# A six-block decoder on one core: its loads and first steps at the edges of the blocks rearranged

## The chip, the core and the metric

The kernel runs on one core of a Trainium2 chip. The core has a matrix engine (PE in the profile, with its weight loads as PEld), a vector engine (DVE), a scalar engine (ACT), GpSimd (POOL) and SyncE (SP), which here only issues DMAs. Each engine works through its own queue of instructions in order. The metric is the device time in microseconds of one execution; lower is better.

## What is computed

The input x holds 16 batches of 256 rows of 256 numbers, all in float32. Six blocks follow one another, each of the form x = x + block(layernorm(x)):

```python
x = x + L0_attn(ln(x))            # block 0: causal attention, 16 heads of 64, with biases bq, bk, bv, bo
x = x + L0_xattn(ln(x), ctx)      # block 1: attention to a context, with an additive mask, 16 heads of 64
x = x + L0_ffn(ln(x))             # block 2: RMS norm, top 2 of 8 experts, x itself added once more inside
x = x + L1_attn(ln(x))            # block 3: causal linear attention, 16 heads of 16
x = x + L1_xattn(ln(x), ctx)      # block 4: softmax attention to the same context, 16 heads of 16, biases
x = x + L1_ffn(ln(x))             # block 5:
#   gates = sigmoid(x @ w_gate), 8 per head; only the first largest is kept (gm)
#   values = einsum('bhne,ehdk,bnd->bhnk', gm, value_experts, x)
#   causal softmax attention over 8 heads of 64 with these values
#   out = einsum('bhne,ehkd,bhnk->bhnd', gm, output_experts, attended), summed over the heads
```

## The kernel before, in words

All rows of x stay in SBUF (xs, one tile of 128 x 2 x 256 for each batch). The weights rotate through three slots of 128 x 8192 floats (pool wp, line 37): first w_a (block 0, wq, wk, wv, wo at columns 0, 2048, 4096, 6144), then w_x, the experts' m_w1 and m_w2, then w34 (lines 733 to 739), which holds the weights of blocks 3 and 4 and block 5's two projections in columns 0 to 6143; columns 6144 to 8191 are unused. The last two are w_ve and w_oe of block 5. A loader of weights is load_rows (line 43), always on SP's queue.

The order in which PE works is written out by hand: each block is a loop of steps over heads and batches, under a manual schedule for PE alone. On every other engine and on SP's queue, the build decides the order from its own estimate of what is ready, with earlier program text first; so a later load may stand ahead of an earlier one in SP's queue. That queue is then fixed, and its head, waiting for a semaphore, holds all behind it.

Each stage opens its own SBUF pool and PSUM pool and closes them at its end (s01 and p01 for blocks 0 and 1, s2 for block 2, s3 for block 3, s4 for block 4, s5 for block 5). The next stage's pool takes the memory of the one before.

Start (lines 54 to 72): SP issues the load of x's first batch, then the four parts of w_a in the order wq, wk, wv, wo (line 52), then the other 15 batches of x, then the biases bq0, bk0, bv0, bq1, bk1 and the gate weights wg, then some more constants, bo0 (line 355) among them. Block 0 begins on PE with the transposes of the first batch (line 189), the values ps_v from wv (line 393), then queries and keys ps_qk (line 408), which ACT copies out with the biases (lines 414 and 417; bq0s is bq0 scaled on DVE, line 107), the scores (line 235), the softmax on DVE and ACT, its normalising on POOL (line 256), and the transposes of the probabilities (line 266). POOL also adds bo0 to each batch of x (line 374).

Block 4 needs keys and values of the context for each batch. They are computed ahead by context4 (line 287), a generator of three parts: load the batch's context ct (line 79), project the keys, copy them on ACT and store them to DRAM (kd), and the same for the values (vd). Two batches (EARLY) are done at the end of block 1, with their stores on ACT's queue. The other 14, called late, are done in block 3, with ct in two slots of the pool vep and their stores on SP's queue. fill (line 306) advances the generators: when one ends, it starts the next but one, which issues that one's load. In block 3, eight parts come before the first step, three in each of the steps -3 to -1 and one in each later step. In the text of step 10 stands load_ffn (line 891), 12 loads for block 5's weights on SP, which wait for a gate that POOL writes into the slots from batch 2's x (line 895).

Block 3 ends with the statistics of the last batch for block 4: output3, stats and rstd_one (lines 1063 to 1073), whose last operations run on POOL (lines 157 to 164).

Block 4 (lines 1126 to 1300) runs 64 sets (batch, m, o) in steps -3 to 68. prepare4 loads k4 and v4 of a batch from kd and vd into tiles of the stage pool s4, and makes the normalised rows; keys4 makes from k4, on ACT, the four masked and biased km (line 1158); project4 makes the queries; scores4 takes scores for the maxima (line 1205, reduced on DVE at 1211), maxima4 adds the maxima to the queries, exps4 takes the scores again (line 1231) and ACT exponentiates them into pT, weighted4 multiplies by the values (line 1244) and finish4 transposes and normalises (lines 1257, 920 and 924). The first DMA of the stage is the bias bv1 (line 1130). statistics5 (line 1264) makes block 5's statistics, on DVE and then POOL.

Block 5 begins with before5(0) (line 1316), in five steps of its own: transposes of the normalised rows to hT, gates on PE (ps_g), a chain of DVE operations with one exponential on ACT (lines 1328 to 1340) to gm, its transposes (line 1345), a copy and a store to DRAM (gd). Only then the first pair5 (line 1353): queries and keys, causal scores (one PSUM buffer for them, so that a pair's scores wait for the pair before to be exponentiated), expert values, and the sums, with gr loaded from gd. For later batches before5 runs beside pair5 of the batch before.

Of the kernel before, what the change touches and what calls it, by code (L numbers as in the profile page):

```python
# [10 lines left out]
F32 = mybir.dt.float32  # L11
# [6 lines left out]
P = 128  # L18
# [7 lines left out]
def decoder(ctx: ExitStack, tc: tile.TileContext, a: dict, out: bass.AP):  # L26
# [21 lines left out]
        return dst  # L48

    def load_attention(which):  # L50
        w = weights(f"w_{which}")
        return [load_rows(w, 2048 * i, f"{which}_{n}") for i, n in enumerate(("wq", "wk", "wv", "wo"))]

    xs = []
    for b in range(NB):
# [2 lines left out]
        xs.append(xb)  # L58
        if b == 0:
            w_first = load_attention("a0")  # L60

    def load_const(name, shape, src):
        t = const.tile(shape, F32, tag=name, name=name)
        nc.sync.dma_start(out=t, in_=src)
        return t

    bq0 = load_const("bq0", [P, 8], a["a0_bq"])
    bk0 = load_const("bk0", [P, 8], a["a0_bk"])
    bv0 = load_const("bv0", [P, 8], a["a0_bv"])
    bq1 = load_const("bq1", [P, 2], a["x1_bq"])  # L70
    bk1 = load_const("bk1", [P, 2], a["x1_bk"])
    wg = load_const("wg", [P, 2, 64], a["f_wg"].rearrange("(c p) e -> p c e", p=P))

    dram = ctx.enter_context(tc.tile_pool(name="dram", bufs=1, space=bass.MemoryType.DRAM))

    def ctx_rows(b, pool):

        ct = pool.tile([P, 2, S], F32, tag="c", name="c", bufs=2)
        nc.sync.dma_start(
            out=ct, in_=a["ctxT"][:, b * S : (b + 1) * S].rearrange("(c p) s -> p c s", p=P)  # L80
        )
        return ct
# [201 lines left out]
    kds = [dram.tile([P, 2, S], F32, tag=f"kd{b}", name=f"kd{b}") for b in range(NB)]  # L284
    vds = [dram.tile([P, 2, D], F32, tag=f"vd{b}", name=f"vd{b}") for b in range(NB)]

    def context4(b, pool, mm, wk, wv, kt, vt, queue, cpool=None):

        ct = ctx_rows(b, cpool or pool)
        yield  # L290
        ps = mm([P, 2, S], "ps_k4")
        for m in range(2):
            two_k(ps[:, m, :], lambda c: wk[:, c, m * P : (m + 1) * P], lambda c: ct[:, c, :])
        k = pool.tile([P, 2, S], F32, tag=kt[0], name="k4", bufs=kt[1])
        nc.scalar.copy(k, ps)
        queue.dma_start(out=kds[b], in_=k)
        yield
        ps = mm([P, 2, D], "ps_v4")
        for t in range(2):
            two_k(ps[:, t, :], lambda c: ct[:, c, t * P : (t + 1) * P], lambda c: wv[:, c, :])  # L300
        v = pool.tile([P, 2, D], F32, tag=vt[0], name="v4", bufs=vt[1])
        nc.scalar.copy(v, ps)
        queue.dma_start(out=vds[b], in_=v)
        yield

    def fill(gens, n):

        for _ in range(n):
            while gens and next(gens[0], 0) == 0:
                gens.pop(0)  # L310
                if len(gens) > 1:
                    next(gens[1])

# [29 lines left out]
    with ExitStack() as st:  # L345
# [338 lines left out]
        with tc.manual_schedule(engines={mybir.EngineType.PE}):  # L684
            prepare(0, 0)
            rows_T(0, 0)
            values(0, 0, 0)
            n = 0
            early = []
            while n < len(duos) + 4 or routing:  # L690
                if n == 2:
                    wts[1] = load_attention("x0")
                    for p in perms:
                        nc.sync.dma_start(out=p.rearrange("(p f) o -> p (f o)", p=P), in_=zero)
                if n == 4 * NB + 4:
                    load_moe()
                if n == len(duos) - 1:
                    w4 = []
                    for name, cols in (("x1_wqk", slice(D, 2 * D)), ("x1_wv", slice(0, D))):
                        w = pool.tile([P, 2, D], F32, tag="v", name="w4", bufs=6)  # L700
                        nc.sync.dma_start(
                            out=w, in_=a[name][:, cols].rearrange("(c p) e -> p c e", p=P)
                        )
                        w4.append(w)
                    early = [
                        context4(b, pool, mm_tile, *w4, ("qk", 2), ("v", 6), nc.scalar)
                        for b in range(EARLY)
                    ]
                    next(early[0])
                    next(early[1])  # L710
                step(n)
                n += 1
            fill(early, 2 * EARLY)
# [16 lines left out]
    with ExitStack() as st:  # L730
# [6 lines left out]
        wxqk = load_rows(w34, 2048, "x1_wqk")  # L737
        wxv = load_rows(w34, 3072, "x1_wv")
        wfqk = [load_rows(w34, 4096, "f_wq"), load_rows(w34, 5120, "f_wk")]

        def once(shape, name, dt=F32):
            return pool.tile(shape, dt, tag=name, name=name, bufs=1)
# [186 lines left out]
    with ExitStack() as st:  # L929
# [133 lines left out]
        def output3(b):  # L1063
# [9 lines left out]
            rstd_one(4, b, pool, nc.gpsimd)  # L1073

        late = [
            context4(b, pool, mm3, wxqk[:, :, D : 2 * D], wxv, ("k4", 2), ("v4", 2), nc.sync, vep)
            for b in range(EARLY, NB)
        ]

# [24 lines left out]
                    values3(b + 1)  # L1104

        with tc.manual_schedule(engines={mybir.EngineType.PE}):
            next(late[0])
            next(late[1])
            combine(0)
            fill(late, 8)  # L1110
            for s in range(-3, len(SETS) + 6):
                step3(s)
                fill(late, 3 if s < 0 else 1)
                if s == 10:
                    load_ffn(xs[2][0:1, 0, 0:32])

    ve_stack.close()
    rt_stack.close()

# [4 lines left out]
    with ExitStack() as st:  # L1126
# [40 lines left out]
            )  # L1167

        def prepare4(b):
            k = pool.tile([P, 2, S], F32, tag="k4", name="k4", bufs=2)  # L1170
            nc.sync.dma_start(out=k, in_=kds[b])
            v = pool.tile([P, 2, D], F32, tag="v4", name="v4", bufs=2)
            nc.sync.dma_start(out=v, in_=vds[b])
            kvs[b] = k, v
            hs4[b] = normed(4, b)

            nc.gpsimd.tensor_tensor(
# [118 lines left out]

        with tc.manual_schedule(engines={mybir.EngineType.PE}):
            prepare4(0)
            for s in range(-3, len(SETS) + 5):
                step4(s)  # L1300

# [3 lines left out]
    with ExitStack() as st:  # L1307
# [3 lines left out]
        wve = [w_ve[:, 2048 * g : 2048 * (g + 1)] for g in range(4)]  # L1311
        wve = [w.rearrange("p (k c f) -> p k c f", k=2, c=2) for w in wve]
        woe = [w_oe[:, 2048 * g : 2048 * (g + 1)].rearrange("p (e d) -> p e d", e=8) for g in range(4)]
        hTs, gms, gds, pos = {}, {}, {}, {}

        def before5(b):
            ps = transposed(normed(5, b), psum, "mm", bufs=3)
            hT = hTs[b] = hp.tile([P, 2, S], F32, tag="hT", name="hT")
            nc.scalar.copy(hT, ps)
            yield 6  # L1320

            ps = psum.tile([P, 2, 64], F32, tag="mm", name="ps_g", bufs=3)
            for t in range(2):
                two_k(ps[:, t, :], lambda c: hT[:, c, t * P : (t + 1) * P], lambda c: wg[:, c, :])
            gt = pool.tile([P, 16, 8], F32, tag="gt", name="gt")
            gtf = gt.rearrange("p a e -> p (a e)")

            nc.vector.tensor_scalar(gtf, ps.rearrange("p t e -> p (t e)"), -80.0, None, ALU.max)
            nc.scalar.activation(gtf, gtf, AF.Exp, scale=-1.0)
            nc.vector.tensor_scalar(gtf, gtf, 1.0, None, ALU.add)  # L1330
            nc.vector.reciprocal(gtf, gtf)
            m = pool.tile([P, 16], F32, tag="m", name="m")
            nc.vector.tensor_reduce(m, gt, AX.X, ALU.max)
            oh = pool.tile([P, 16, 8], F32, tag="oh", name="oh")
            nc.vector.tensor_tensor(oh, gt, m.unsqueeze(2).to_broadcast([P, 16, 8]), ALU.is_equal)
            nc.vector.tensor_tensor(oh, oh, rev.unsqueeze(1).to_broadcast([P, 16, 8]), ALU.mult)
            nc.vector.tensor_reduce(m, oh, AX.X, ALU.max)
            nc.vector.tensor_tensor(oh, oh, m.unsqueeze(2).to_broadcast([P, 16, 8]), ALU.is_equal)
            gm = gms[b] = pool.tile([P, 2, 8, 8], F32, tag="gm", name="gm")
            nc.vector.tensor_tensor(gm.rearrange("p t h e -> p (t h) e"), oh, gt, ALU.mult)  # L1340
            yield 6
            yield 6
            ps = psum.tile([64, 2, P], F32, tag="mm", name="ps_gT", bufs=3)
            for t in range(2):
                nc.tensor.transpose(
                    ps[:, t, :], gm[:, t, :, :].rearrange("p h e -> p (h e)"), ident
                )
            gmT = pool.tile([64, S], F32, tag="gmT", name="gmT")
            nc.scalar.copy(gmT, ps.rearrange("p t s -> p (t s)"))
            gd = gds[b] = dram.tile([64, S], F32, tag="gd", name="gd", bufs=2)  # L1350
            nc.sync.dma_start(out=gd, in_=gmT)

        def pair5(b, hp):
            hT, gm = hTs[b], gms[b]
            cols = slice(hp * P, (hp + 1) * P)
            ps = psum.tile([P, 2, S], F32, tag="mm", name="ps_qk", bufs=3)
            for i in range(2):
# [8 lines left out]
            for j in range(2):  # L1366
                h = 2 * hp + j
                nc.sync.dma_start(
                    out=gr[64 * j : 64 * j + 64].rearrange("p e s -> p (e s)"),
                    in_=gds[b][8 * h : 8 * h + 8, :]  # L1370
                    .rearrange("e s -> (e s)")
                    .partition_broadcast(64),
                )
# [44 lines left out]
                nc.sync.dma_start(out=out[b].rearrange("(t p) d -> p t d", p=P), in_=xs[b])  # L1418

        def steps5():  # L1420
            yield [(6, before5(0))]
            for _ in range(4):
                yield []
            for b in range(NB):
                for hp in range(4):
                    new = [(3, pair5(b, hp))]
                    if hp == 2 and b + 1 < NB:
                        new.append((6, before5(b + 1)))
                    yield new

        with tc.manual_schedule(engines={mybir.EngineType.PE}):
# [75 lines left out]
```

## Time and profile before

| | us |
|---|---|
| median of 3 runs | 3912.89 (3911.7 to 3913.84) |
| the profiled execution, device time | 3917.66 |
| its span, from its first to its last instruction | 3916.0 |
| PE busy in the span | 3759.0 |
| DVE, ACT, POOL busy | 2248.7, 1616.7, 1039.2 |

The profile's times come from the one profiled execution and are counted from the span's start. In a list in order of time each line gives the start, the duration of the group, the engine, the line of the kernel, the operation, output and inputs by the program's names, and in brackets how long the engine had been idle and what released it; "issue" there means that nothing the profile shows was waited for. A line with SPq or ACTq is a DMA's issue on that queue. In the chain of work that ended last, each line gives start, duration and what it was. In a table by stage, each engine's busy time follows the stretch and its length, and at the end come the granted clock of PE, the share of DMA time and GB/s. Block 3 begins at about 2017, block 4 at about 2384, block 5 at about 2719. From 2770 to 3890 PE is busy all the time.

### The profile page before, as it was taken

How to read it: one execution, taken by the hardware profiler on the slowest of the kernel's cores; microseconds unless marked ns; L12 is line 12 of the kernel's file. 1: busy time of each engine (PE TensorE's matmuls, PEld its weight loads, DVE VectorE, ACT ScalarE, POOL GpSimd, SP SyncE). 2: the span in 40 equal slices, each digit the busy share in tenths (PEclk: the TensorE clock that was granted, in tenths of full speed). 3: DMA queues.
4: the chain of work that ended last, by engine and by line, in shares of the span. 5: the costliest groups of instructions: out<-in, count | busy, mean ns of one | idle time of the engine just before them, and what ended most of it. 6: DMA issues, size and time to landing. Idle time of an engine off the chain costs nothing.

```text
span 3916.0 us, 63635 instructions
## 1 busy us (share of the span) xinstructions
PE 3759.0 (96%) x23088; PEld 2679.1 (68%) x23088; DVE 2248.7 (57%) x6215; ACT 1616.7 (41%) x4876; POOL 1039.2 (27%) x1472
## 2 busy tenths in 40 slices
PE   8999999999999999979989888998999999999999
PEld 6777776777777776756667665665666666666666
DVE  5666667645556555522234765776655555555554
ACT  4555554555555555423335555665212212212211
POOL 3332332333344334322224653221100000000000
PEclk9999999999999999979999999999999999999999
DMA  5000000010000000032234001001222222222222
GB/s 192 1 1 1 1 1 1 1 57 17 9 17 17 17 9 17 17 89 65 64 122 146 28 17 35 25 26 24 56 64 58 65 64 58 65 64 58 66 63 49
DMA packets 88456, 171.65 MB, mean 44 GB/s; under 512 B 12480, under 2 KB 60744, under 8 KB 79952
## 3 DMA queue, kind: packets, MB, share of 16 engines
q1 hardware_dynamic: 78992, 148.65, 13.9%
q0 software_dynamic: 8576, 17.87, 1.7%
q8 instruction: 186, 3.05, 0.3%
q10 hardware_dynamic: 576, 1.05, 0.1%
q14 instruction: 126, 1.03, 0.1%
HBM read 139.70 MB, written 27.82 MB: 43 GB/s over the span
## 4 chain that ended last, share of the span: by engine, by line
PE 86%; DVE 9%; issue 2%; ACT 1%; DMA 1%; POOL 1%; SPq 0%; another core or an unknown queue 0%; ACTq 0%; DVEq 0%; POOLq 0%
PE ps_qk L197 14%; PE po L1412 11%; PE ps_ve L197 11%; PE ps_v L197 6%; PE tr L266 6%; PE po L503 6%; PE sc L235 4%; PE ps_h L197 3%; PE po L877 3%; PE av L272 3%; PE sc L431 2%; PE av L488 2%; PE sc L1231 2%; PE sc L1205 2%; PE zt L1244 1%
## 5 line engine op out<-in xcount | busy, mean ns | idle before, releaser
L256 POOL TENSOR_TENSOR pr<-pr,sm 128x256 f32<-128x256 f32 (+1 forms) x384 | 309.7, 827 | 1444.2 <-DVE sm L254 1337.5
L250 ACT ACTIVATE pr<-sc,nmx 128x128 f32<-128x128 f32 (+1 forms) x768 | 314.7, 417 | 348.1 <-DVE nmx L248 311.9
L1412 PE MATMUL po<-w_oe,ut 128*128 128x256 f32 x2048 | 452.4, 379 | 0.0
L197 PE MATMUL ps_ve<-w_ve,hT 128*128 128x512 f32 x1024 | 450.8, 593 | 0.0
L1412 PEld LDWEIGHTS po<-w_oe,ut 128*128 128x128 f32 x2048 | 388.8, 190 | 52.8 <-issue 0.2
L267 ACT COPY pT<-tr 128x512 f32<-128x512 f32 (+1 forms) x256 | 135.9, 531 | 650.2 <-PE tr L266 650.2
L266 PEld LDWEIGHTS tr<-ident,pr 128*128 128x128 f32 x2176 | 270.8, 141 | 168.5 <-issue 117.5
L266 PE MATMUL tr<-ident,pr 128*128 128x128 f32 x2176 | 346.8, 275 | 14.1 <-ACT zT L497 11.2
L452 POOL TENSOR_TENSOR pr<-pr,sm 128x512 f32<-128x512 f32 x256 | 264.2, 1053 | 286.8 <-DVE sm L450 176.4
L446 ACT ACTIVATE pr<-sc,nmx 128x256 f32<-128x256 f32 x512 | 236.7, 470 | 250.8 <-DVE nmx L441 172.3
L197 PEld LDWEIGHTS ps_ve<-w_ve,hT 128*128 128x128 f32 x1024 | 191.1, 190 | 215.3 <-issue 207.1
L1384 DVE TENSOR_TENSOR tv<-ps_ve,gm 128x512 f32<-128x512 f32 x256 | 176.4, 689 | 204.7 <-PE ps_ve L197 198.2
L441 DVE CUSTOM_DVE_ANT_0 sc<-sc,mk 128x256 f32<-128x256 f32 x512 | 211.0, 443 | 112.6 <-PE sc L431 59.5
L248 DVE TENSOR_REDUCE nmx<-sc 128x2 f32<-128x256 f32 (+1 forms) x384 | 208.2, 556 | 111.0 <-ACT pr L250 106.2
L197 PE MATMUL ps_qk<-hT,w_a 128*128 128x256 f32 x1024 | 260.0, 387 | 0.0
L267 DVE COPY pT<-tr 128x384 f32<-128x384 f32 (+1 forms) x384 | 223.0, 594 | 19.2 <-PE tr L266 12.9
L197 PEld LDWEIGHTS ps_qk<-hT,w_a 128*128 128x128 f32 x1024 | 180.8, 191 | 29.7 <-issue 11.8
L197 PE MATMUL ps_qk<-hT,w 128*128 128x256 f32 x768 | 194.0, 398 | 0.0
L866 DVE COPY hs<-ps_h 128x512 f32<-128x512 f32 x72 | 49.8, 691 | 223.0 <-PE ps_h L197 223.0
L1211 DVE TENSOR_REDUCE nm<-sc 128x4 f32<-128x1024 f32 x128 | 150.9, 1221 | 43.2 <-PE sc L1205 43.2
L235 PE MATMUL sc<-qk 64*128 64x128 f32 (+1 forms) x1536 | 163.4, 346 | 8.6 <-ACT qk L417 6.2
L197 PEld LDWEIGHTS ps_qk<-hT,w 128*128 128x128 f32 x768 | 147.5, 203 | 19.4 <-issue 1.2
(279 smaller groups left out, 7010.4 us busy)
## 6 DMA issues: line engine op xcount, KB each, us to landing
gr<-gd SPq DMA_DIRECT2D x128, 512.0 KB
yd<-y SPq DMA_DIRECT2D x72, 128.0 KB
c<-in_ctxT SPq DMA_DIRECT2D x32, 256.0 KB
m_w<-in_m_w SPq DMA_DIRECT2D x16, 512.0 KB
x<-in_x SPq DMA_DIRECT2D x16, 256.0 KB
mk<-in_mask SPq DMA_DIRECT2D x16, 256.0 KB
hd<-h SPq DMA_DIRECT2D x16, 256.0 KB
w_ve<-in_f_ve SPq DMA_DIRECT2D x8, 512.0 KB
```

The costliest lines, as they stand in the source:

```text
L197: nc.tensor.matmul(ps, lhsT=lhsT(c), rhs=rhs(c), start=(c == 0), stop=(c == 1))
L235: nc.tensor.matmul(sc[:, j, at : at + ks], lhsT=qk[rows, 0, qs], rhs=qk[rows, 1, 0:ks], start=True, stop=True,)
L248: nc.vector.tensor_reduce(nmx[:, qt, :], sc[:, :, sl], AX.X, ALU.max, negate=True)
L250: nc.scalar.activation(pr[:, j, sl], sc[:, j, sl], AF.Exp, bias=nmx[:, qt, j : j + 1], accum_out=sm[:, qt, j : j + 1],)
L256: nc.gpsimd.tensor_tensor(pr[:, :, sl], pr[:, :, sl], sm[:, qt, :].unsqueeze(2).to_broadcast([P, 2, n]), ALU.mult,)
L266: nc.tensor.transpose(tr[:, at : at + P], src, ident)
L267: copy(pT, tr[:, 0 : P * len(blocks)])
L441: nc.vector.tensor_tensor_reduce(out=sc[:, j, t, :], in0=sc[:, j, t, :], in1=mk[:, t, :], scale=-1.0, scalar=3.4e38, op0=ALU.add, op1=ALU. ...
L446: nc.scalar.activation(pr[:, j, t, :], sc[:, j, t, :], AF.Exp, bias=nmx[:, j, t : t + 1], scale=-1.0, accum_out=sm[:, j, t : t + 1],)
L452: nc.gpsimd.tensor_tensor(pr[:, j], pr[:, j], sm[:, j, :].unsqueeze(2).to_broadcast([P, 2, S]), ALU.mult)
L503: nc.tensor.matmul(po, lhsT=zTs[l, b, c][:, t * P : (t + 1) * P], rhs=wts[l][3][:, c, :], start=(c == 0), stop=(c == 7),)
L1412: nc.tensor.matmul(po[:, t, :], lhsT=ut[:, e, t * P : (t + 1) * P], rhs=woe[hp][:, e, :], start=(hp == 0 and e == 0), stop=(hp == 3 and e ...
```

## The change

- At the start, the parts of w_a are loaded in the order wv, wq, wk, wo, and bq0, bk0, bv0 are issued on ACT's queue, in the text right after w_a's loads.
- In block 3, the stores of the late keys and values go to ACT's queue, so that SP has of context4 only the loads of ct; ct has three slots instead of two, three loads are started at once, and fill starts the next but two.
- Block 4's loaded keys and values take the unused columns 6144 to 8191 of w34 (two sets of them) instead of tiles in s4.
- before5 moves out of block 5; its tiles come from a pool gp that is opened before block 4's pool. For batch 0 it is called in block 4 with block 4's PSUM tiles, a part in each of the steps 64 to 67 (and at 68, where it has ended); block 5 starts with pair5 at once.

```diff
     def load_attention(which):
         w = weights(f"w_{which}")
-        return [load_rows(w, 2048 * i, f"{which}_{n}") for i, n in enumerate(("wq", "wk", "wv", "wo"))]
+        at = {n: load_rows(w, 2048 * i, f"{which}_{n}") for i, n in enumerate(("wv", "wq", "wk", "wo"))}
+        return [at[n] for n in ("wq", "wk", "wv", "wo")]
...
         if b == 0:
             w_first = load_attention("a0")
-    bq0 = load_const("bq0", [P, 8], a["a0_bq"])
-    bk0 = load_const("bk0", [P, 8], a["a0_bk"])
-    bv0 = load_const("bv0", [P, 8], a["a0_bv"])
+            bq0 = load_const("bq0", [P, 8], a["a0_bq"], nc.scalar)
+            bk0 = load_const("bk0", [P, 8], a["a0_bk"], nc.scalar)
+            bv0 = load_const("bv0", [P, 8], a["a0_bv"], nc.scalar)
...
-    def context4(b, pool, mm, wk, wv, kt, vt, queue, cpool=None):
-        ct = ctx_rows(b, cpool or pool)
+    def context4(b, pool, mm, wk, wv, kt, vt, cpool=None):
+        ct = ctx_rows(b, cpool or pool, 3 if cpool else 2)
...
-        queue.dma_start(out=kds[b], in_=k)
+        nc.scalar.dma_start(out=kds[b], in_=k)
...
-        queue.dma_start(out=vds[b], in_=v)
+        nc.scalar.dma_start(out=vds[b], in_=v)
...
-    def fill(gens, n):
+    def fill(gens, n, ahead=1):
         for _ in range(n):
             while gens and next(gens[0], 0) == 0:
                 gens.pop(0)
-                if len(gens) > 1:
-                    next(gens[1])
+                if len(gens) > ahead:
+                    next(gens[ahead])
...
+        kv34 = [
+            [w34[:, at : at + 512].rearrange("p (c s) -> p c s", c=2) for at in (6144 + i, 6656 + i)]
+            for i in (0, 1024)
+        ]
...
-            next(late[0])
-            next(late[1])
+            for g in late[:3]:
+                next(g)
             combine(0)
-            fill(late, 8)
+            fill(late, 8, 2)
             for s in range(-3, len(SETS) + 6):
                 step3(s)
-                fill(late, 3 if s < 0 else 1)
+                fill(late, 3 if s < 0 else 1, 2)
...
+    gp = ctx.enter_context(tc.tile_pool(name="gp", bufs=2))
+    hTs5, gms5, gds5 = {}, {}, {}
+    def before5(b, mm):
...
         def prepare4(b):
-            k = pool.tile([P, 2, S], F32, tag="k4", name="k4", bufs=2)
-            nc.sync.dma_start(out=k, in_=kds[b])
-            v = pool.tile([P, 2, D], F32, tag="v4", name="v4", bufs=2)
-            nc.sync.dma_start(out=v, in_=vds[b])
-            kvs[b] = k, v
+            kvs[b] = kv34[b % 2]
+            for at, src in zip(kvs[b], (kds[b], vds[b])):
+                nc.sync.dma_start(out=at, in_=src)
...
             prepare4(0)
+            first5 = before5(0, mm4)
             for s in range(-3, len(SETS) + 5):
                 step4(s)
+                if s >= len(SETS):
+                    next(first5, None)
...
         def steps5():
-            yield [(6, before5(0))]
-            for _ in range(4):
-                yield []
             for b in range(NB):
```

The body of before5 is otherwise as before, with its tiles in gp and its PSUM tiles from the function it is given.

## The prediction

> **What bounds the kernel now.** I read the page's busy times first, then the busy time by stage, and then, at each of the four places that the change touches, the chain of work that ended last and the instructions in order of time.
>
> ```profile
> PE 3759.0 (96%) x23088; PEld 2679.1 (68%) x23088; DVE 2248.7 (57%) x6215; ACT 1616.7 (41%) x4876; POOL 1039.2 (27%) x1472
> ```
>
> ```profile
> 0.00:40.00 40.00, 23.35 (x92) 15.68 (x93) 18.64 (x77) 9.38 (x31) 11.86 (x64) 0.91 0.93 325
> ...
> 2000.00:2060.00 60.00, 49.06 (x209) 38.55 (x209) 25.20 (x94) 19.06 (x42) 19.80 (x22) 0.91 0.55 178
> 2060.00:2120.00 60.00, 59.64 (x526) 46.66 (x525) 23.04 (x68) 33.76 (x70) 18.60 (x24) 1.00 0.56 197
> ...
> 2360.00:2420.00 60.00, 45.11 (x444) 29.29 (x439) 30.42 (x72) 25.46 (x48) 21.05 (x55) 0.91 0.12 38
> ...
> 2690.00:2770.00 80.00, 64.55 (x437) 38.78 (x430) 45.14 (x108) 27.94 (x67) 14.71 (x45) 0.87 0.14 30
> 2770.00:3890.00 1120.00, 1120.00 (x4958) 766.42 (x4957) 643.01 (x1147) 226.27 (x770) 98.70 (x122) 1.00 0.27 63
> ```
>
> PE sets the time (first number after the length; the last three are granted clock, DMA share, GB/s): the last block is PE without a gap. Only the edges have room: PE is idle for 17 of the first 40 us, 11 us where block 3 begins, 15 us where block 4 begins, 15 us where block 5 begins. The change removes no matmul, so it can win only there.
>
> **Start (A).** In order of time:
>
> ```profile
> 11.62 3.69 PE L197 MATMUL ps_v<-w_a,hT 128*128 128x512 f32 x4 [2.77 <-DMA w_a<-in_a_wv]
> ...
> 25.48 0.17 DVE L107 TENSOR_SCALAR bq0s<-bq 128x8 f32<-128x8 f32 x1 [2.20 <-DMA bq<-in_a_bq]
> ...
> 26.65 2.93 PE L235 MATMUL sc<-qk 64*128 64x128 f32 x16 [6.16 <-ACT qk L417]
> ...
> 30.68 4.14 POOL L374 TENSOR_TENSOR x<-x,bo 128x256 f32<-128x256 f32 x6 [25.02 <-DMA bo<-in_a_bo]
> ```
>
> PE waits 2.77 for wv, then 6.16 for a bias that SP issues only at 19.69, behind 15 loads of x. With wv first it lands at about 3.6 + 2.6 (the four 1 MB weights end at 14.2, x at 3.6: 2.65 each), before hT at 9.5; wq and wk land by 11.6 as wv did. ps_v and the projections then run from 9.5 without a stop: 6.9 us at full clock plus half of what falls in the slow clock until about 15.1, so 19.2. The first scores start there and not at 26.65: 7.4. They and the next projections then find the full clock (2.93 becomes the 1.58 of the scores at 36.19; 5.03 becomes 3.5): up to 9.5. What is late next is POOL: its six x + bo wait for bo0, and the first probabilities are normalised behind them. SP issues three loads fewer (0.65 each), so bo0 lands near 28.7, POOL is free at 32.9, and the first transpose (39.31 now) can start at 33.7: 5.6. If the build queues the normalising ahead, it is 9.3. I take **7 (5.5 to 9.5)**. The three bias issues on ACT cost 0.33 each, hidden, since ACT's first copy comes at 8.89[...]; were bq0s queued on DVE ahead of the first statistics, up to 3 of the 7 would go.
>
> **Block 3 begins (B).** The chain there:
>
> ```profile
> 2037.01 7.68 issue
> 2044.70 0.38 SPq L899
> ...
> 2045.68 4.82 DMA c<-in_ctxT
> 2050.51 0.77 issue
> 2051.28 3.75 PE ps_k L197 x8
> ```
>
> SP's queue is in order. After a key store at 2036.63 its head is the first 512 KB load of the last block's weights, which waits for its gate until 2044.70; the context of batch 8, whose slot was free at 2037.7, waits behind it. PE stands from 2042.84 to 2051.28 and then runs the slow clock (3.75 where 1.89 is usual, 2.62 for 1.89): 8.44 + 2.6 = 11. The third slot lets batch 8's context go after batch 5's values (2033.2), ahead of the gate: it is there in time. But batch 9's now takes the place behind the gate: issued at 2045.2, landing near 2050, wanted at 2048.2 (batch 8's 3.6 and the 1.9 of ps_v after 2042.84); batch 10's comes behind two more weight loads, where a store now holds SP for 2.81, near 2054 to 2057, wanted at 2053.7. So 2 to 5 of the 11 come back. The earlier waits of 0.63 and 0.78 for contexts win nothing, since the transposes at 2033.08 start on DVE's h, made at 2033.05. **7 (3 to 11).**
>
> [...] The 7.68 is time at the queue's head[...]; I credit that[...].
>
> The stores' issues (28, one per 3.6 us at first, then one per step of some 5) go to ACT. A store there costs:
>
> ```profile
> 1694.77 0.33 ACTq L296 DMA_DIRECT2D kd<-k  x1
> ```
>
> 28 x 0.35 (with the wait for its own copy) is 9.8 us of ACT time, behind which its exponentials and score copies queue. ACT is busy 33.8 of 60 us in the dense stretch and idle over 1 us per step, so I book **-0.5 (0 to -9)**; with that cover gone all 9.8 is lost.
>
> **Block 4 begins (C).**
>
> ```profile
> SPq L1130 <- DVE rsq_k L153: 78.0, 1, 78.0
> ```
>
> ```profile
> 2389.31 0.33 SPq L1130 DMA_DIRECT2D bv<-in_x_bv  x1
> 2389.32 1.02 ACT L1192 ACTIVATE q<-ps_q,bq1h,halvesq 128x256 f32<-128x256 f32 x2 [4.07 <-POOL rstd L164]
> ...
> 2395.03 2.09 PE L1205 MATMUL sc<-km,q 32*128 32x256 f32 x16 [8.59 <-DMA k<-kd]
> ```
>
> bv, q and the memsets of nm all start when POOL's last rstd of block 3 ends (2389.29): I read that as the release of the whole stage pool. Keys and values wait for the same release and then 5 us for their landing. In the unused end of the w34 slot they need no release and can land during block 3. But km and q, still in the stage pool, cannot: ACT starts at 2389.3, four km (0.505 each) and half of q (0.51) give scores at 2391.9, with q first 2391.0. Gain 3.1 to 4.0, and up to 2 more if the shorter gap spares the slow clock (2.09 for 1.15). **4 (0 to 6)**; 0 if these loads are queued on SP behind bv, which stood there 78 us.
>
> **Block 5 begins (D).**
>
> ```profile
> 2725.79 0.29 DVE L1328 TENSOR_SCALAR gt<-ps_g 128x128 f32<-128x128 f32 x1 [3.34 <-POOL rstd L164]
> ...
> 2729.71 0.61 PE L1345 MATMUL ps_gT<-ident,gm 128*64 128x128 f32 x2 [8.05 <-issue]
> ...
> 2733.77 0.38 ACT L1360 ACTIVATE qk<-ps_qk 128x256 f32<-128x256 f32 x1 [3.05 <-PE ps_qk L197]
> ...
> 2741.12 0.93 PE L235 MATMUL sc<-qk 64*128 64x128 f32 x8 [1.66 <-ACT pr L250]
> ```
>
> Now gt waits for the release of block 4's pool (2725.76), the gate chain takes 3.9, and the first projection stands behind gT. Moved into the last steps of block 4, the four transposes (0.63), eight gate matmuls (1.1) and two gT (0.61) fill PE's waits for the exponentials (0.58 to 0.80 + 0.29 a step); they shift the tail by 0.4. DVE adds 3.3, ACT three small operations (1.25), SP one store, all in idle stretches. gT then runs at about 2721 and the first projection at 2722, 8 us sooner. But its ACT copy writes a block 5 tile, which needs the same release: 2725.76 plus 0.4 to 1.5 for the shift and the gates on DVE, so 2726.5 for 2733.77: 7.3. Behind it the scores wait 4 to 5 us for the first softmax as now. **8 (6 to 12)**; 12 if the tile needs no release.
>
> [...] The trace already has clock 0.50 over 2730.11 to 2733.73 and fell before the 8.05 gap was over, after a stretch half busy; so I take slow, with 0.7 credited.
>
> **Sum.** 7 + 7 - 0.5 + 4 + 8 = 25.5. The profiled execution took 3917.66 (span 3916.0), so 3892 in its own terms; against the median 3912.89 that is **3887.4**. Elsewhere the matmul order is unchanged.
>
> **Rivals.** (1) The queues keep their order: weights stay ahead of the contexts and the loads of keys behind bv. B and C give nothing: 7 + 8 - 0.5 = 14.5, 3898. For it: SP's 7.68 and 78.0. Against: the build already places weight loads between contexts. (2) Nothing new is late: 9.5 + 11 + 5.5 + 11 = 37, 3876. Against: POOL's 25.02 and the two releases. (3) Slower: the slot w34 is guarded as a whole, so that each load of keys and values waits for PE's projections from it and the next projection for the load: 4.3 in flight + 0.86 issue = 5.2 in each of 14 later batches, 72 less 22, 3963. It decides from five batches on. Against: PE read wv's part of w_a at 11.62 while wo's part landed at 14.2. (4) The stores on ACT stand in the path, and B goes with them: 7 - 9.8 + 4 + 8 = 9.2, 3904; against it speaks ACT's idle share.
>
> **How the numbers follow.** Likeliest case 0.68, rival 1 0.14, rival 2 0.12, rival 3 0.03, rival 4 0.03. The range 3877 to 3898 takes the likeliest case's ends and half of rivals 1 and 2. Beyond 0.2% (7.8 us, about what a measurement can tell): faster 0.93, same 0.04 (the low ends of rivals 1 and 4), slower 0.03.
>
> **What would show it.** Scores at 19 to 20 in A, with POOL's x + bo ahead of the first transpose; no wait for batch 8's context but one for batch 9 or 10; loads from kd before bv, and scores near 2391.5 less what A and B won; gT in block 4's tail, and the first qk of block 5 released by POOL's rstd. I am wrong if those POOL waits are absent, if PE loses time between 2055 and 2125, or if block 4 waits for key loads in each batch.

## The result, and the profile after

The changed kernel takes 3889.63 us (median of 5 runs, 3888.64 to 3895.15) where the kernel before takes 3913.42 in the same comparison (5 runs, 3911.7 to 3913.95): a ratio of 0.9942, 95% interval 0.9928 to 0.9957, or 23.8 us less. The forecast was 3887.4, and 25.5 less. The profiled execution took 3889.63 (span 3887.8), so it is typical; the one of before, 3917.66, was not, and the two profiles differ by 28.2. Where the 4 us between 28.2 and 23.8 went is shown by the other kernels below.

First the page's busy times, then the stretches that were shown of before (length, then PE, PEld, DVE, ACT, POOL busy, granted clock, DMA share, GB/s):

```profile
PE 3753.4 (97%) x23088; PEld 2679.3 (69%) x23088; DVE 2249.9 (58%) x6215; ACT 1615.7 (42%) x4876; POOL 1039.6 (27%) x1472
```

```profile
0.00:40.00 40.00, 28.47 (x130) 18.92 (x132) 24.27 (x86) 14.13 (x47) 15.15 (x68) 1.00 0.97 346
2000.00:2060.00 60.00, 52.63 (x278) 42.67 (x277) 27.47 (x98) 23.92 (x48) 24.04 (x26) 0.97 0.78 267
2060.00:2120.00 60.00, 58.45 (x554) 45.30 (x556) 26.11 (x81) 35.40 (x74) 24.58 (x31) 1.00 0.32 114
2360.00:2420.00 60.00, 48.51 (x458) 30.95 (x460) 35.01 (x71) 29.92 (x49) 18.14 (x48) 0.91 0.10 29
2690.00:2770.00 80.00, 72.54 (x366) 44.79 (x367) 51.25 (x112) 24.01 (x76) 15.25 (x36) 0.96 0.24 55
```

PE does the same 23088 matmuls. It is idle for less of each edge (11.5 of the first 40 us where it was 17, 7.5 of 80 at block 5 where it was 15), and the granted clock is higher at all edges but the begin of block 4, where it is 0.91 in both.

**Start.** In order of time:

```profile
9.49 3.78 PE L198 MATMUL ps_v<-w_a,hT 128*128 128x512 f32 x4 [0.67 <-ACT hT L386]
...
19.48 1.58 PE L236 MATMUL sc<-qk 64*128 64x128 f32 x16
...
25.21 1.64 POOL L257 TENSOR_TENSOR pr<-pr,sm 128x256 f32<-128x256 f32 x2 [19.52 <-DVE sm L255]
...
30.37 2.78 POOL L375 TENSOR_TENSOR x<-x,bo 128x256 f32<-128x256 f32 x4
...
31.62 0.49 PE L267 MATMUL tr<-ident,pr 128*128 128x128 f32 x3
```

The scores stand at 19.48 (forecast 19.2). POOL normalises first and adds the biases behind: the wait that I had put in this place, and whose absence I had named as a sign of being wrong, is absent. The first transpose is 7.9 us sooner than at 39.53 before.

**Block 3 begins.** PE waits for a context after all, and ACT's ks stands still longer (line L1009 is its new number):

```profile
2039.43 3.65 PE L198 MATMUL ps_k<-c,w 128*128 128x256 f32 x8 [2.45 <-DMA c<-in_ctxT]
...
2042.11 0.91 ACT L1009 ACTIVATE ks<-qk,halves 128x256 f32<-128x256 f32 x2 [9.68 <-DVE qk L1006]
2042.92 0.56 ACT L296 COPY k<-ps_k 128x512 f32<-128x512 f32 x1
...
2053.72 0.56 ACT L303 COPY v<-ps_v 128x512 f32<-128x512 f32 x1
2055.57 0.33 ACTq L304 DMA_DIRECT2D vd<-v  x1
2055.94 0.80 ACT L1029 COPY at<-sc 128x768 f32<-128x768 f32 x1 [1.65 <-DMA c<-in_ctxT]
...
2056.79 1.20 PE L1020 MATMUL sc<-qk,ks 32*128 32x256 f32 x16 [1.81 <-ACT at L1029]
```

The last wait comes from one of the moved stores. The copy of v ends at 2054.28, its store is issued only at 2055.57, and ACT's copy of scores, for which PE waits, stands behind it. What the issue waited for is not shown beyond the label. With the last block's weights loaded later (below) the same copy of v ends at 2054.79, its store goes out at 2054.81, and this wait of PE is absent.

**Block 4 begins.** ACT starts when POOL's last rstd of block 3 has ended, as forecast, and the bias load comes behind the key loads:

```profile
2373.13 0.19 POOL L165 TENSOR_TENSOR rstd<-rsq_t,rsq_k 128x2 f32<-128x2 f32 x1
2373.35 0.34 SPq L1183 DMA_DIRECT2D bv<-in_x_bv  x1
2373.36 2.07 ACT L1211 ACTIVATE km<-w,bk1h,halves 128x256 f32<-128x256 f32 x4 [4.07 <-POOL rstd L165]
2375.34 1.00 ACT L1243 ACTIVATE q<-ps_q,bq1h,halvesq 128x256 f32<-128x256 f32 x2
...
2375.98 2.09 PE L1256 MATMUL sc<-km,q 32*128 32x256 f32 x16 [5.51 <-ACT q L1243]
```

PE's wait is 5.51 where it was 8.59.

**Block 5 begins.** The gates' transposes stand in block 4's tail, and ACT's first copy of queries is released by POOL's rstd:

```profile
2703.21 0.38 PE L1165 MATMUL ps_gT<-ident,gm 128*64 128x128 f32 x2 [2.69 <-DVE gm L1160]
2704.04 2.79 PE L198 MATMUL ps_qk<-hT,w 128*128 128x256 f32 x8 [0.46 <-ACT gmT L1169]
2707.88 0.38 ACT L1380 ACTIVATE qk<-ps_qk 128x256 f32<-128x256 f32 x1 [3.89 <-POOL rstd L165]
2708.63 1.65 PE L236 MATMUL sc<-qk 64*128 64x128 f32 x8 [1.79 <-POOL rstd L165]
```

### The profile page after: what moved, and what is told of

Its sections match the earlier page's. It is cut to its first block, busy times and chain, and to the rows that moved or that the text cites. A ratio compares the mean times of both kernels' runs of the same rounds, so it can differ in the third digit from the quotient of the medians.

```text
span 3887.8 us, 63585 instructions
## 1 busy us (share of the span) xinstructions
PE 3753.4 (97%) x23088; PEld 2679.3 (69%) x23088; DVE 2249.9 (58%) x6215; ACT 1615.7 (42%) x4876; POOL 1039.6 (27%) x1472
## 4 chain that ended last, share of the span: by engine, by line
PE 85%; DVE 10%; issue 1%; ACT 1%; DMA 1%; POOL 1%; SPq 0%; ACTq 0%; DVEq 0%; POOLq 0%
PE ps_qk L198 14%; PE po L1432 11%; PE ps_ve L198 11%; PE ps_v L198 6%; PE tr L267 6%; PE po L504 6%; PE sc L236 4%; PE ps_h L198 3%; PE po L883 3%; PE av L273 3%; PE sc L432 2%; PE av L489 2%; PE sc L1256 2%; PE sc L1282 2%; PE zt L1295 1%
## 5 line engine op out<-in xcount | busy, mean ns | idle before, releaser
L267 PEld LDWEIGHTS tr<-ident,pr 128*128 128x128 f32 x2176 | 270.8, 141 | 167.5 <-issue 116.6
L1262 DVE TENSOR_REDUCE nm<-sc 128x4 f32<-128x1024 f32 x128 | 150.9, 1221 | 41.2 <-PE sc L1256 41.2
```

What stands on the lines that cost most here:

```text
L267: nc.tensor.transpose(tr[:, at : at + P], src, ident)
```

## The experiments

Twelve kernels: each of the four parts alone on the kernel before, the two halves of B alone, and six with edits of their own. For all of them the same places on PE were read from the first and last starts of a tile's matmuls: the last scores of block 1; then from the last ps_h of block 2 to the last ps_k (begin of block 3), to the first ps_q (steady part of block 3), to the last ps_q (block 4), to the first ps_ve (begin of block 5). What the table leaves out is the same in all: 367.8 to 369.0 from block 1's end to the last ps_h, and 1142.1 or 1142.2 from the first ps_ve to the last. The time is the median, with the ratio to before and its interval.

| kernel | block 1 ends at | begin of 3 | rest of 3 | block 4 | begin of 5 | time | ratio |
|---|---|---|---|---|---|---|---|
| before | 1642.8 | 104.3 | 269.5 | 307.3 | 53.3 | 3913 | 1 |
| changed | 1633.0 | 99.1 | 269.3 | 305.4 | 43.1 | 3889.6 | 0.9942 (0.9928 to 0.9957) |
| A alone | 1633.1 | 104.2 | 270.9 | 308.7 | 51.1 | 3906.3 | 0.9983 (0.9976 to 0.9990) |
| B alone | 1639.4 | 100.5 | 267.9 | 308.3 | 51.3 | 3909.6 | 0.9994 (0.9986 to 1.0003) |
| C alone | 1639.2 | 104.1 | 270.6 | 304.1 | 51.3 | 3908.4 | 0.9989 (0.9982 to 0.9996) |
| D alone | 1638.0 | 103.4 | 270.7 | 307.1 | 43.6 | 3903.3 | 0.9976 (0.9966 to 0.9986) |
| B, slots only | 1638.3 | 99.7 | 271.0 | 307.4 | 53.3 | 3909.1 | 0.9990 (0.9981 to 0.9998) |
| B, stores only | 1638.3 | 100.7 | 270.8 | 308.6 | 51.2 | 3909.4 | 0.9992 (0.9984 to 1.0000) |
| before + qk ahead | 1638.8 | 94.3 | 253.9 | 308.8 | 51.1 | 3883.0 | 0.9923 (0.9909 to 0.9936) |
| changed + weights later | 1632.6 | 98.6 | 271.0 | 304.0 | 43.7 | 3891.0 | 0.9941 (0.9928 to 0.9955) |
| changed + qk ahead | 1632.8 | 96.1 | 253.3 | 304.7 | 45.5 | 3871.7 | 0.9892 (0.9877 to 0.9907) |
| changed + both | 1631.3 | 94.2 | 251.9 | 306.1 | 43.7 | 3870.6 | 0.9893 (0.9878 to 0.9909) |
| changed + own pool | 1632.2 | 106.0 | 266.1 | 296.8 | 43.6 | 3884.7 | 0.9928 (0.9914 to 0.9942) |
| changed + all three | 1631.8 | 91.8 | 309.0 | 297.4 | 45.7 | 3916.9 | 1.0010 (1.0001 to 1.0018) |

The table places the 4 us: in the six other kernels with the start of before, block 1 ends at 1638.0 to 1639.4 (mean 1638.7). The profiled execution of before alone is at 1642.8. So of the 9.8 between the two profiles in this column some 4 belong to that one execution, and 5.7 are the start.

**Each part alone.** A is the start of the diff shown above, B the slots and the stores, C the kv34 slot, D before5 in block 4.

> The kernel before with the start alone changed (wv first, three biases on ACT's queue). Prediction: 7 us less (5.5 to 9.5), about 3906. Theory of the two profiles (the steps of the last block 1 stand 9.9 us earlier after the change): about 10 us less, 3903.5, and the 3.6 us beyond the 6.3 won by 40 us belong to the start. Rival: those 3.6 us are chance of the two profiled executions (the one of before was 4.2 us over its median), so that the start gives about 6.3, 3907, and nothing more is won between 40 and 1676 us.

Measured: 6.7 less. The rival held: 5.6 sooner at the end of block 1, nothing more after that.

> The kernel before with block 3's edge alone changed (three slots for the contexts, stores of keys and values on ACT's queue). Prediction: 6.5 us less, about 3907. Theory of the two profiles: 5.3 us less, 3908: the wait of 8.4 for batch 8's context goes, 2.5 for batch 9's and 1.8 for a score buffer come in its place. Rival (the issues on ACT cost what they win): within 2 us of before.

Measured: 3.3 less by the medians, with an interval that includes no change; 3.5 in its own stretch against the mean of 104.0 of the kernels without a change at this edge. PE waits 3.94 for a context there. This is less than forecast; why is asked below.

> The kernel before with block 4's edge alone changed (its keys and values in the unused end of the weights' slot). Prediction: 4 us less, about 3909.4. Theory of the two profiles: 3.0 at the first scores, of which 1 is given back to a slower clock behind them, so 2 less, 3911.4, hardly to be told from before. Rival: the time given back comes from something else that waits at this edge (the release by POOL), then 3 to 4 less as the clock falls otherwise.

Measured: 4.6 less by the medians, 3 to 4 in its own stretch. The prediction held.

> The kernel before with block 5's edge alone changed (gates of the first batch made in block 4's tail). Prediction: 8 us less, about 3905.4. Theory of the two profiles: 10 us less, 3903.4 (8.0 at ACT's first copy of the queries and 2.2 more as the clock recovers sooner). Rival: part of the 10 belongs to the other edges[...], and alone it gives 8 or less. Its blocks 0 to 3 are those of before, so their profile also shows how far two executions of the same code differ.

Measured: 9.6 less by the medians, 8.2 in its own stretch against the mean of 51.8 of the kernels without D. Between the forecast and the reading of the two profiles. The four medians add up to 24.2, the whole change wins 23.8: within the noise the parts add up.

**The halves of B.** The first is the c tiles in three slots, with the stores as before. The second is one word:

```
-            context4(b, pool, mm3, wxqk[:, :, D : 2 * D], wxv, ("k4", 2), ("v4", 2), nc.sync, vep)
+            context4(b, pool, mm3, wxqk[:, :, D : 2 * D], wxv, ("k4", 2), ("v4", 2), nc.scalar, vep)
```

> The kernel before with three slots for the contexts, the stores of keys and values still on SP's queue. Theory of DVE's order: the wait for batch 8's context is only covered by ACT's ks, which ends near 2051 in any case, so the slot wins what both parts won, 3 less at most, and stores and slots together are no more than one of them: about 3910. Theory of the queue (as predicted): with the stores on SP the contexts stand behind them and the gate, so the slot alone wins 2 or less, 3911 to 3913.

> The kernel before with the stores of keys and values on ACT's queue, the contexts still in two slots. If ACT's issues cost something on the path (rival 4 of the prediction, 9.2 in all): slower than before, up to 3922. If they are hidden and SP's queue runs freer: 0 to 3 less, 3910 to 3913.

Measured: 4.7 and 4.4 less, and both parts together 3.3. Either half wins all that B wins, but not in the same way. With the stores alone the context of batch 8 still stands behind the gate, and PE still waits for it:

```profile
2044.29 3.63 PE L197 MATMUL ps_k<-c,w 128*128 128x256 f32 x8 [6.82 <-DMA c<-in_ctxT]
```

That is 1.9 sooner after the last ps_h than before. The context is issued 0.46 behind the first weight load where it was 0.98, because no store stands between them, and it is 4.21 in flight where it was 4.82; the values behind it take 1.89 for 2.62. In this run no store holds ACT, and the 28 issues (0.33 each) cost nothing that could be seen, so rival 4 falls. The one store that held ACT in the changed kernel is the exception.

With the slots alone, in order of time on PE and on ACT:

```profile
2046.02 3.75 PE L197 MATMUL ps_k<-c,w 128*128 128x256 f32 x8 [3.67 <-ACT ks L1003]
```

```profile
2037.24 0.58 ACT L302 COPY v<-ps_v 128x512 f32<-128x512 f32 x1 [0.47 <-ACT qk L999]
2045.08 0.91 ACT L1003 ACTIVATE ks<-qk,halves 128x256 f32<-128x256 f32 x2 [7.26 <-DVE qk L1000]
2045.90 0.56 ACT L295 COPY k<-ps_k 128x512 f32<-128x512 f32 x1
```

PE's row names ks, but this needs care: ps_k does not read ks, and its PSUM buffer had been free since 2037.82. What it waits for is its context, issued by SP at 2040.54; with the median of 5.4 in flight here it lands at about 2045.9, as ks ends. That two things end together is the finding. ACT's ks waits 7.26 for DVE's qk, and behind ks stands the copy that frees a PSUM buffer (mm3 has four, in turn) for the product after this one, till 2046.46. In the kernel before the same ks came at 2050.39 (DVE, then ACT):

```profile
2049.67 0.68 DVE L1000 SCALAR_TENSOR_TENSOR qk<-ex,qk 128x512 f32<-128x512 f32 x1
2050.39 0.91 ACT L1003 ACTIVATE ks<-qk,halves 128x256 f32<-128x256 f32 x2 [4.31 <-DVE qk L1000]
```

The inputs of qk were ready at 2042.9 (ACT's relu at 2042.35 took 0.59), but DVE was then working through statistics and sums of two later batches, from 2040.97 on. Had the context been in time and this order the same, PE could have made four more products, to 2049.8, and would then have waited for a buffer till ks and the first copy were over, 2051.9. By this estimate, from the times of these rows, 2.1 of the wait cannot be won by any earlier context.

**Contexts or DVE's order.** Two edits on the changed kernel tell them apart, alone and together. The first loads the last block's weights after batch 4's sum:

```
-                if s == 10:
-                    load_ffn(xs[2][0:1, 0, 0:32])
+                if s == 26:
+                    load_ffn(xs[4][0:1, 0, 0:32])
```

The second queues the sums and statistics of batch b behind the first qk of batch b - 2 on DVE; first_qk[b] is filled where project3 makes qk:

```
         def combine(b):
             with ExitStack() as order:
                 if last:
                     order.enter_context(tc.issue_after(last[-1]))
+                if b >= 2:
+                    order.enter_context(tc.issue_after(first_qk[b - 2]))
```

> The changed kernel (3889.6) with the last block's weights loaded after the sum of batch 4 in block 3 instead of at step 10's place[...]. Theory of the prediction (the contexts of batches 9 and 10 behind the gated weights are what is late next): the wait of 2.45 for a context and part of the slow clock behind it go, 3 to 5 less, about 3885.5. Rival (ACT's ks stands 9.7 us for DVE's qk, which is queued behind the sums and statistics of two later batches; six copies of keys and values stand behind it, and PE runs out of its four PSUM buffers): PE stops at the same place on a buffer instead of a context, within 1.5 us of 3889.6.

Measured: 3891.0, no gain. PE waits for no context at this edge, and stops for a buffer instead, which ACT's copy behind ks frees (PE, then ACT):

```profile
2043.32 2.61 PE L198 MATMUL ps_v<-w,c 128*128 128x256 f32 x8 [2.35 <-ACT k L296]
```

```profile
2041.89 0.91 ACT L1009 ACTIVATE ks<-qk,halves 128x256 f32<-128x256 f32 x2 [7.21 <-DVE qk L1006]
2042.71 0.56 ACT L296 COPY k<-ps_k 128x512 f32<-128x512 f32 x1
```

The rival held: the wait only changed its name.

> The changed kernel (3889.6) with DVE's order at the begin of block 3 altered: the sums and statistics of batch 2 are queued behind the first qk of batch 0, those of batch 3 behind the first of batch 1. Theory of DVE's order: ks starts some 9 us sooner and ACT's copies with it; the wait for the context of batch 9 stays, so 1 to 3 less, about 3887.5. Theory of the contexts: nothing, since the context ends the wait last; 3889.6. If the sums now come too late for their own rows, PE waits for h in the steps of batch 2: 1 to 3 more.

> The changed kernel with both: weights later and qk ahead. If each alone leaves the other's wait, both together win what neither wins alone: the 2.45, 0.45 and 1.81 of waits and some 2 us of slow clock, 4 to 6 less, about 3884.6. If only the contexts matter, it equals the run with the weights later; if only DVE's order matters, it equals the run with qk ahead.

Measured: 3871.7 and 3870.6, 18 and 19 less than the changed kernel. With qk ahead ACT's ks no longer waits for DVE:

```profile
2035.11 0.91 ACT L1013 ACTIVATE ks<-qk,halves 128x256 f32<-128x256 f32 x2 [0.40 <-DVE qk L1009]
```

At the begin of block 3 qk ahead wins 3.0, and both 4.9, as expected. That the steady part falls from 269.3 to 253.3 was not foreseen by any theory written down. PE's waits of 2120 to 2340 us, changed kernel first, then with qk ahead (total, times, longest):

```profile
PE sc L1020 <- ACT at L1029: 23.9, 11, 2.4
```

```profile
PE sc L1024 <- ACT at L1033: 17.9, 19, 2.4
```

In the changed kernel they come about once for each batch, 2.2 each. In one of them DVE makes the statistics of a later batch first (2142.0 to 2147.2), its qk at 2147.60, and ACT's ks and copies of scores come behind, so that the scores at 2149.96 wait 2.18. With qk ahead the waits are shorter and 6 less in sum. The rest is the clock: over the whole steady part PE is idle for 23.4 where it was 30.3, and the same matmuls keep it busy for 229.9 where it was 239.0, at a granted clock of 0.99 for 0.95. So of the 16.0 some 7 are waiting and 9 are slower matmuls. Not every wait has a slow clock behind it: in the changed kernel the granted clock is 0.50 from 2170 to 2172, behind the wait of 1.99 before 2168.37, but still 1.00 from 2147 to 2169, behind the wait of 2.18 before 2149.96.

> The kernel before with only DVE's order in block 3 altered (sums and statistics of batch b+2 queued behind the first qk of batch b). With the changed kernel it won 18: some 3 at the begin of block 3 and some 15 in its steady part (score buffers waited for 23.9 us in 11 places of 2.2 each, one for each batch[...]). Theory: the steady 15 do not need the change, the 3 at the begin do (the context of batch 8 is still 8.4 late): 13 to 16 less, 3897 to 3900. Rival: the steady gain [...]needs the change: 5 or less.

Measured: 3883.0, 30.8 less than before and more than the whole change wins. The steady part does not need the change (253.9), and neither does the begin of block 3: its 94.3 is as good as the 94.2 of the changed kernel with both edits. With qk ahead the keys are copied and stored without a halt, the build also puts the weights later in SP's queue, and the context waits of 9.2 shrink to 3.0 in three places:

```profile
2048.22 1.97 PE L197 MATMUL ps_k<-c,w 128*128 128x256 f32 x8 [1.20 <-DMA c<-in_ctxT]
```

So this edit changed both orders at once, and B adds nothing to it (96.1 with the whole change, 94.3 without).

**The release by POOL.** At the begins of blocks 4 and 5 ACT waited for an rstd that it does not read. The edit gives those statistics a pool of their own, sp, opened beside the weights' pool:

```
-            stats(4, b, pool)
-            rstd_one(4, b, pool, nc.gpsimd)
+            stats(4, b, sp)
+            rstd_one(4, b, sp, nc.gpsimd)
...
-                stats(5, b, pool)
-                rstd_one(5, b, pool, nc.gpsimd)
+                stats(5, b, sp)
+                rstd_one(5, b, sp, nc.gpsimd)
```

> The changed kernel (3889.6) with the statistics that blocks 3 and 4 make for the next block in a pool of their own, not in the stage's pool. Theory of the release: ACT's km in block 4 waits 4.07 and ACT's first qk in block 5 waits 3.89 for POOL's rstd only because that one still uses memory of the stage that ends; with it elsewhere both start up to 4 us sooner, and what PE waits at the first scores falls by 3 to 4 in block 4 and by 2 to 3.5 in block 5 (the softmax chain there has its own 1.7): 5 to 7 less, about 3883.5. Rival: other memory of the stage is released just as late, or the waits go over to the next operation: within 1.5 us of 3889.6.

Measured: 3884.7, 5.0 less, but made up otherwise than expected. Block 4 wins 8.6: PE's first scores wait 0.81, and take 1.15 for 2.09. (The last rows are of block 5's begin.)

```profile
2374.93 1.15 PE L1257 MATMUL sc<-km,q 32*128 32x256 f32 x16 [0.81 <-ACT q L1244]
...
2698.34 0.38 PE L1166 MATMUL ps_gT<-ident,gm 128*64 128x128 f32 x2 [2.69 <-DVE gm L1161]
2699.18 3.60 PE L199 MATMUL ps_qk<-hT,w 128*128 128x256 f32 x8 [0.46 <-ACT gmT L1170]
```

```profile
2702.95 0.38 ACT L1381 ACTIVATE qk<-ps_qk 128x256 f32<-128x256 f32 x1 [3.83 <-PE ps_qk L199]
```

Block 5 wins nothing: ACT's first copy comes 4.6 after gT, as in the changed kernel (4.7), released now by PE's own projection. In the changed kernel that projection had ended at 2706.83, 1.0 before the release by POOL. Here it takes 3.60 for 2.79, and these 0.8 took back what the earlier release gave. The steady part of block 3 wins 3.2. And the begin of block 3 loses 7: its order changed too, and one context is in flight for 12.13 beside the weights (the chain of work):

```profile
2036.83 12.13 DMA c<-in_ctxT
```

> The changed kernel with weights later, qk ahead, and the statistics of blocks 3 and 4 in a pool of their own. Qk ahead and weights later gave 3870.6; the pool alone won 5, though the begin of block 3 lost 7 there to a context of 12 us in flight beside the weights. In block 4 it won 7 to 8.6. Theory: with the weights out of the way the 7 are not lost, so 7 to 9 less than 3870.6: about 3862.5. Rival: the gains share the same slow clock, 3866.

Measured: 3916.9, worse than all others, though it differs from the kernel with both edits (3870.6) only by the pool. The begin of block 3 is the best of all (91.8) and block 4 keeps its gain (297.4), but the rest of block 3 takes 309.0. PE's waits of 2120 to 2380 us:

```profile
PE sc L1025 <- ACT at L1033: 44.6, 10, 4.8
```

```profile
2177.65 0.37 ACT L1033 COPY at<-sc 128x256 f32<-128x256 f32 x1 [6.85 <-DVE at L1032]
```

The build put the statistics of a later batch ahead of the masked scores at (L1032) on DVE, so that ACT's copy stands 6.85. The steady part takes 57 more than with both edits (309.0 for 251.9): PE is idle for 28.7 more, and busy for 28.4 more with the same matmuls. From 2100 to 2340 us its granted clock is 0.86, where with qk ahead alone it is 0.99. In the same 240 us DVE is busy for 172.7 with 490 operations of all shapes, 0.35 each, where with qk ahead alone it is 179.7 with 598, 0.30 each; so longer DVE operations are a rival to their order (see the last section). Which of the two costs how much was not tried.

## Why the prediction was right or wrong, point by point

- **The time** was 2.2 above the forecast and inside the likeliest case; direction and size held. Terms of the sum against the parts alone: A 7 against 6.7, B 6.5 (7 less 0.5 for ACT) against 3.3, C 4 against 4.6, D 8 against 9.6. That the sum is so close is in part luck: B fell short by 3.2, and C and D together gave 2.2 more than their terms.
- **A, right in size, wrong in what is late next.** The first scores came at 19.48 for 19.2. The step "late next is POOL", 5.6, failed: the build queued the normalising ahead, which the prediction had priced at 9.3. Only 6.3 of that was left at the scores behind the first transposes (38.89 for 45.16), because PE waits for ACT and DVE at 28.93, 34.62 and 36.21 (1.65, 0.45, 1.07). The 7 was taken between the two branches, and the one that came fell 3 short of its price, so that the closeness is luck. The steps to "up to 9.5" add up to 10.3; at the values behind the next projections 9.8 had come (24.55 for 34.38). bq0s on DVE cost nothing: it starts at 3.51, when its bias has landed. The forecast's slow clock until about 15.1 was the author's estimate, from the 3.69 of ps_v before (1.88 later). The changed kernel's first matmuls were slow too, ps_v with 3.78 and the projections behind it with 4.76 (3.72 for the next 16), but the granted clock in the records is 1.00 from 7 to 19.48, so what slowed them is not shown.
- **B, the term that was mis-sized.** For the contexts the mechanism was right: batch 8's is in time, batch 9's late by 2.45 (3.94 with B alone; forecast 2 to 5 in all). What failed is that nothing but contexts was priced as coming back. DVE's qk does not come sooner when the contexts do (38.2 after the last ps_h before, 40.5 with the weights later); so ACT's ks, the copies behind it and PE's buffers set the end, and with no context late at all nothing more is won. The trace of before showed it in ACT's row of ks with 4.31 of waiting, which the prediction does not mention. B alone won 3.3; in its own stretch it won 3.5, and 4.9 beside the other parts (99.1 for a mean of 104.0), where 6.5 was booked.
- **The head of SP's queue, credited in B.** The stores' move alone won 4.4 (0 to 6), but not at that head: with the stores on ACT it still waits 10.8 for the gate, with batch 8's context behind it. Of the 1.9 by which that context became less late, 0.5 is issue time. The credit for the head belongs to the third slot.
- **Stores on ACT, -0.5:** not to be seen with the stores alone. In the changed kernel one store stood 1.29 before its issue, and PE waited 1.81 behind it, more than was booked.
- **C, right.** km and q did wait for the stage pool's release, and 3.1 came at the scores. That the release was the limit is shown by the run that removed it: the first scores' wait fell from 5.51 to 0.81, and the block took 8.6 less.
- **D, right, 1.6 low.** The copy of queries stood 8.0 sooner (33.2 after block 4's last projection of queries in D alone, 41.2 before; forecast 7.3). The rest is the clock: before, the first scores took 1.65 at a granted clock of 0.50 and the second projection 3.41 at 0.57, and in D alone they took 0.93 and 2.00; in the changed kernel the second took 2.82 at 0.70 and the third 2.00 at 1.00. The 0.7 credited for it was the author's estimate; the scores alone gave that (1.65 less 0.93). The first projection took 2.79 in the changed kernel after a gap of 2.69, and 3.49 in D alone after a gap of 2.68, where eight such matmuls took 1.89 before, at a granted clock of 1.00 (ps_v at 2040.95). In the changed kernel the granted clock was still 1.00 through the gap and fell only behind it, to 0.69 on average over the projection. In the 3.5 before the projection PE did no more than the 0.38 of gT. So here the shorter gap, 2.69 for 8.05, did not leave the clock at 1.00. The named release by POOL was real, and last by 1.0 in the changed kernel, but the run without it won nothing there.
- **The rivals.** SP's order did change, which the first had denied. New waits did come, against the second. Block 4 is no slower than before, so the third, with the slot guarded as a whole, falls. The stores alone cost nothing, against the fourth.

## What to carry to other kernels

When a late transfer is removed, ask what else was about to stop the same engine: read, for every engine that feeds it, the row that ends last before the wait is over, even if that engine counts as idle. An in-order queue (here DVE's statistics of later batches ahead of one small operation, with ACT's copies behind that) can hold more than the transfer that hides it: one forced order was worth 30.8 alone, all four edges together 23.8. And after any edit that moves memory or text, read the order of the other engines again, since the build decides it anew: three edits, of which one changed nothing and two won, gave 3916.9 together, more than before any change.

## What the runs showed of the hardware

Executions of the same text can stand 4 us apart (block 1 ended at 1642.8 in one kernel and at 1638.7 on average in the six others whose blocks 0 and 1 are written alike). So a difference of two profiles can be taken as the worth of an edge only beside other kernels with the same text there. And on DVE an operation of 128x2, 0.16 to 0.19 in the rows around, took 1.80 and 1.85 in the last kernel, ending each time within 0.03 of the end of POOL's multiplication of at (1.28 and 1.27):

```profile
2170.56 1.80 DVE L173 TENSOR_SCALAR rs_v<-mv 128x2 f32<-128x2 f32 x1
...
2174.20 1.85 DVE L161 SCALAR_TENSOR_TENSOR rsq_t<-rsq_t,rs_v 128x2 f32<-128x2 f32 x1
```

The POOL rows of that stretch are at 2171.05 and 2174.75. A wait of one engine for the other would fit these times, but no run shows it.
